# A prologue reordered: the context made during the softmax, the sums of B by TensorE, spare products in TensorE's first pauses, and all loads behind the first x1 on one queue

## The chip, the cores and the metric

The kernel runs on one core of a Trainium2 chip. All arithmetic is float32. The metric is the device time of one execution, in microseconds (us), as the median of several runs. Beside that, one execution was recorded by the profiler; every duration below comes from that record, with times counted from the start of its span.

## The reference, cut to what matters

The input is x with 128 batch rows, 64 channels and 1024 positions, and a conditioning vector of 128 numbers for each batch row. Two layers follow each other, each added to x.

```python
# layer 0
h   = gelu(gelu(cond @ W0 + b0) @ W1 + b1)
att = softmax(h @ W2 + b2)                        # 128 batch rows x 8
agg_w, agg_b = att . weight, att @ bias_k         # a 64x64 matrix and 64 biases for each batch row
z   = agg_w @ x + agg_b                           # for each batch row
x   = x + z @ (A @ B.T).T + ffn_bias              # rank 128
# layer 1
y   = grouped_conv(x, 9 taps, 4 groups) + cond @ c_weight.T + fside      # the middle term is the "context"
x   = x + y @ W_up + the low-rank part of the expert that a gate picks (4 experts, rank 8)
```

The product with B comes first in the kernel: x B is 128 columns wide, the 64x64 matrices act on that, and A widens it again. A bias agg_b that is constant along the positions becomes, after B, agg_b times the column sums of B. That is what the "sums of B" are for.

## The kernel before

Two batch rows make a pair (128 partitions: 64 channels twice), and there are 64 pairs. For each pair, `layer0_in` multiplies the transposed x by B (eight 128x128 products into `pxb`), `layer0_mix` multiplies by a block matrix with the two 64x64 matrices (`pz`), and `layer0_out` multiplies by A (two 128x512 products into `pd`), adds x on VectorE, writes the result to a scratch in DRAM (`x1d`, two transfers) and reads it back shifted into a tile `X` (two transfers), on which the convolution works. `conv_in` makes the convolution for one batch row of a pair (`pc`), and `conv_out` adds the context and writes `yt`. Two pairs make one step d of the last layer: `ffn_a`, `ffn_sums` and `ffn` multiply `yt` by W_up in seven products of sub-blocks (`w11`, `w12`, `w21`, `w22` and the sums T1 to T4 of them that `w_sum` makes).

The engines' instruction orders are written by hand: each engine runs its instructions in the order of the program text, and waits in place for what it needs. Every engine that issues DMAs (SP, ScalarE as ACT, and GpSimd as POOL) issues them in that order too. SP and ACT each have one queue, and POOL has one.

The prologue is the part before the loop over d. It reads the packed parameters (`pk`), B, the x of pair 0, A and others; makes `att` in `condition`; and carries the first four pairs (FIRST = 4) through layer 0 with block matrices that VectorE builds itself from `att` and the weights (`own_att`: a product `pattx` that turns `att` for the pair; `own_bd`: eight steps on VectorE; `own_bias`: the biases, with `attT` from `turn_att`). For all later pairs, `agg_all` makes the 64x64 matrices of all batch rows with eight products, and `agg_out` writes them to DRAM, from where `load_cond` reads them group by group (a group is two pairs). `load_cond` also broadcasts agg_b and the context of the group to all partitions; before, both lie in one scratch, `smalld`, in a tile `bc`, and `condition_rest` makes them. `b_sums` makes the column sums of B with two products from `bred`, a reduction of B over its eight chunks on VectorE (line 598).

Lines that matter later: 197 and 205 (the first products of `condition`), 228 and 232 (`b_sums`), 241 (`pattx`), 220 (`attT`), 258 (steps of the block matrix), 307, 317, 340 (`pxb`, `pz`, `pd`), 341 (x added), 342 (x1d written), 345 and 346 (X read), 187 (`bc` read), 406 (convolution of pairs 0 and 1), 442 (products with W_up), 369 and 370 (differences for the later pairs' convolution, on POOL), 556 (the bias added to x). The main text of the prologue before reads, around pair 0:

```python
    layer0_mix(0, sums_of_b)
    own_att(1)
    own_bd(1)
    small = condition_rest()
    own_bias(1)
    load_x(2, nc.scalar)
    nc.sync.dma_start(smalld, small)
    layer0_out(0)
    load_cond(0)
    load_cond(1)
```

Of the kernel before, what the change touches and what calls it, by code (L numbers as in the profile page):

```python
# [44 lines left out]
GP = 2  # L45
# [23 lines left out]
def block(ctx: ExitStack, tc: tile.TileContext, a: dict, out: bass.AP):  # L69
# [21 lines left out]
    def bank(name):  # L91
        return ps.tile([P, 512], F32, tag="bank", name=name)
# [7 lines left out]
    ident = const.tile([P, P], F32, name="ident")  # L100
    make_identity(nc, ident)

    xs, xts, bds, bcs = {}, {}, {}, {}

    def load_x(pr, eng=nc.gpsimd):
        xts[pr] = xtp.tile([P, NC, P], F32, tag="xt", name=f"xt{pr}")
# [65 lines left out]
    fold = const.tile([P, GL], F32, name="fold")  # L172
    nc.vector.tensor_tensor(fold, ident[:, :GL], ident[:, GT : GT + GL], ALU.add)
    aggd = dram.tile([NB, CH, CH], F32, name="aggd")
    smalld = dram.tile([NB, 2, CH], F32, name="smalld")

    def load_cond(g):

        if g * GP >= FIRST:
            bds[g] = BD[g % NBD]  # L180
            for b in range(2):
                nc.sync.dma_start(
                    bds[g].rearrange("(r two) t b o -> two r t b o", two=2)[b, :, :, b, :],
                    aggd.rearrange("(t two) r o -> two r t o", two=2)[b, :, g * GP : (g + 1) * GP],
                )
        bcs[g] = bcp.tile([P, GP, 2, 2, CH], F32, tag="bc", name=f"bc{g}")
        nc.sync.dma_start(
            bcs[g].rearrange("p t b k o -> p (t b k o)"),
            smalld[2 * g * GP : 2 * (g + 1) * GP]
            .rearrange("b k o -> (b k o)")  # L190
            .unsqueeze(0)
            .partition_broadcast(P),
        )

    def mlp(w, h, b, name):
        p = bank(f"p{name}")
        nc.tensor.matmul(p[:, :NB], w, h, start=True, stop=True)
        o = const.tile([P, NB], F32, tag=name, name=name)
        nc.scalar.activation(o, p[:, :NB], AF.Gelu, bias=b)
        return o  # L200

    def condition():
        h = mlp(w1, mlp(w0, condT, b0, "h0"), b1, "h1")
        p = bank("plogit")
        nc.tensor.matmul(p[:, :8], h, w2, start=True, stop=True)
        lg = const.tile([P, 8], F32, name="lg0")
        nc.vector.tensor_tensor(lg, p[:, :8], b2, ALU.add)
        nmx = const.tile([P, 1], F32, name="nmx")
        nc.vector.tensor_reduce(nmx, lg, AX.X, ALU.max, negate=True)
        ex = const.tile([P, 8], F32, name="ex")  # L210
        nc.scalar.activation(ex, lg, AF.Exp, bias=nmx)
        sm = const.tile([P, 1], F32, name="sm")
        nc.vector.tensor_reduce(sm, ex, AX.X, ALU.add)
        rs = const.tile([P, 1], F32, name="rs")
        nc.vector.reciprocal(rs, sm)
        nc.vector.tensor_scalar(att[:, :, :8], ex.unsqueeze(1).to_broadcast([P, 4, 8]), rs, None, ALU.mult)

    def turn_att():
        p = bank("pattT")
        nc.tensor.transpose(p[:, :P], att.rearrange("p j k -> p (j k)"), ident)  # L220
        nc.scalar.copy(attT, p[:, :P])

    bred = const.tile([P, P], F32, name="bred")

    def b_sums():

        p = bank("pbs8")
        nc.tensor.matmul(p[:8, :P], ones[:, :8], bred, start=True, stop=True)
        nc.scalar.copy(bs8, p[:8, :P])
        yield  # L230
        p = bank("pbsum")
        nc.tensor.matmul(p[:, :1], bred, ones[:, :1], start=True, stop=True)
        nc.scalar.copy(bsum, p[:, :1])
        yield
# [26 lines left out]
    attT = const.tile([P, NB], F32, name="attT")  # L261
    bsum = const.tile([P, 1], F32, name="bsum")

    def condition_rest():

        p = bank("psmall")
        nc.tensor.matmul(p[:, :CH], attT[:8, :], bk, start=True, stop=True)
        nc.tensor.matmul(p[:, CH : 2 * CH], condT, cwT, start=True, stop=True)
        small = const.tile([NB, 2, CH], F32, name="small")
        nc.scalar.copy(small[:, 0], p[:, :CH])  # L270
        nc.vector.tensor_tensor(small[:, 1], p[:, CH : 2 * CH], fs, ALU.add)
        return small

    aggs = []

    def agg_all():

        first = ytp.tile([NB, 4, 512], F32, tag="yt", name="agg0")
        second = [xpool.tile([NB, 2, 512], F32, tag="x", name=f"agg1{j}") for j in range(2)]
        to = aggd.rearrange("b i o -> b (i o)").rearrange("b (j h n) -> h b j n", j=4, h=2)  # L280
        aggs.extend([(to[0], first), (to[1][:, :2], second[0]), (to[1][:, 2:], second[1])])
        for h in range(2):
            ps4 = [psb.tile([P, N], F32, tag=f"pb{j}", name=f"pagg{h}_{j}") for j in range(4)]
# [13 lines left out]
            nc.sync.dma_start(to, agg)  # L297


    xbs, z0s, yts, opened = {}, {}, {}, {}  # L300
    diffs, pms, m2s, pcs = {}, {}, {}, {}

    def layer0_in(pr):
# [5 lines left out]
        nc.scalar.copy(xb, pxb[:, :P])  # L309
        xbs[pr] = xb  # L310

    def layer0_mix(pr, between=None):
# [5 lines left out]
        if between:  # L318
            next(between)
        z0 = z0p.tile([P, P], F32, tag="z0", name=f"z0_{pr}")  # L320
        to = z0.rearrange("k (o b) -> k b o", b=2)
        pzv = pz[:, :P].rearrange("k (b o) -> k b o", b=2)
        if own:
            nc.tensor.matmul(pz[:, :P], bs8, mv[pr].rearrange("k b o -> k (b o)"), start=False, stop=True)
            nc.scalar.copy(to, pzv)  # L325
        else:
            nc.vector.scalar_tensor_tensor(to, bcs[g][:, t, :, 0, :], bsum, pzv, ALU.mult, ALU.add)
        z0s[pr] = z0

    def layer0_out(pr):  # L330
        x, z0 = xs[pr], z0s.pop(pr)
        xt = X[pr % NX]
        d = x1d.tile([Q, P, P], F32, tag="x1d", name=f"x1d{pr}")
        dv = d.rearrange("q (c g) m -> (q c) g m", g=BG)
        h = P // 2
        for hf in range(2):
            cols = slice(hf * 512, (hf + 1) * 512)
            qs = slice(hf * Q // 2, (hf + 1) * Q // 2)
            pd = bank(f"pd{pr}_{hf}")
            nc.tensor.matmul(pd, z0, at[:, cols], start=True, stop=True)  # L340
            nc.vector.tensor_tensor(x[:, cols], pd, x[:, cols], ALU.add)  # L341
# [13 lines left out]
        return v.rearrange("m (g q o) -> m g q o", g=NGC, q=Q)  # L355

    def context(pr, b, rows=slice(0, P)):
        v = bcs[pr // GP][rows, pr % GP, b, 1, :].rearrange("m (g o) -> m g o", g=NGC)
        return v.unsqueeze(2).to_broadcast([v.shape[0], NGC, Q, GC])

    def differences(pr):
# [269 lines left out]
    lb = loaded("lb", [P, N])  # L631
    next(agg)
    own_att(2)
    own_bd(2)
    own_bias(2)
    conv(0)
# [140 lines left out]
```

## Time and profile before

| | |
|---|---|
| median of 3 runs | 1360.44 us (1358.38 to 1361.58) |
| the profiled execution | 1360.38 us, span 1358.6 us |
| TensorE (PE) busy | 1336.9 us, 98% of the span |
| VectorE (DVE), POOL busy | 586.8 us, 622.1 us |
| granted TensorE clock, mean | 0.997 |
| DMA | 189.64 MB, mean 140 GB/s |
| PE busy in 0 to 10, 10 to 20, 20 to 30, 30 to 40 us | 4.28, 10.00, 7.78, 5.58 us |
| PE busy from 200 to 1300 us | 1100.00 us |

PE is TensorE's multiplying, PEld its loading of weights, which runs beside it. A row of the timeline gives the start, the length of a run of like instructions, the engine, the line, the tiles, the shape, and in brackets how long the engine was idle before and what released it. A product in float32 is recorded as two matmuls. A DMA row gives the time from issue to landing at its end. The difference of 1.8 us between the profiled execution's own time and its span lies around the span.

### The profile page before, as it was taken

The page shows a single profiled execution, that of the slowest core. Times are in us where ns is not written, and L with a number is a line of the kernel's source. Part 1 is how long each engine was busy: PE and PEld are TensorE (multiplying, and loading weights), DVE is VectorE, ACT ScalarE, POOL GpSimd, SP SyncE. Part 2 cuts the span into 40 slices and gives each one's busy share as a digit, 9 for nine tenths or more (in the row PEclk, how much of TensorE's full clock was granted, in tenths as well). Part 3 has the DMA queues.
Part 4 walks back from the last instruction along what each step waited for, and adds up shares of the span by engine and source line. Part 5 has one row for each costly group of instructions (what it writes and reads, how often), then busy time and mean ns, then how long its engine had stood idle before and what let it go on. Part 6 is the DMA issues. An engine that isn't in the chain of part 4 may idle for free.

```text
span 1358.6 us, 18209 instructions
## 1 busy us (share of the span) xinstructions
PE 1336.9 (98%) x7279; PEld 757.6 (56%) x7279; DVE 586.8 (43%) x980; ACT 142.4 (10%) x310; POOL 622.1 (46%) x553
## 2 busy tenths in 40 slices
PE   6999999999999999999999999999999999999997
PEld 4655555555455555555555555555555554555553
DVE  6554344344344444343443343443443443444442
ACT  2011011011011011011010111010110110110100
POOL 2454555344554344554345554445553445543322
PEclk9999999999999999999999999999999999999999
DMA  8854454534445444445434545343544344454220
GB/s 297 268 198 134 108 160 134 155 124 125 121 146 154 141 133 118 134 134 165 139 119 128 139 135 164 125 133 107 160 136 152 124 127 123 142 157 142 70 79 31
DMA packets 179541, 189.64 MB, mean 140 GB/s; under 512 B 16640, under 2 KB 148096, under 8 KB 179072
## 3 DMA queue, kind: packets, MB, share of 16 engines
q1 hardware_dynamic: 160592, 119.25, 31.2%
q0 software_dynamic: 17712, 65.02, 13.9%
q10 hardware_dynamic: 1152, 4.19, 0.9%
q8 instruction: 58, 0.95, 0.3%
q14 instruction: 27, 0.22, 0.1%
HBM read 119.16 MB, written 69.27 MB: 139 GB/s over the span
## 4 chain that ended last, share of the span: by engine, by line
PE 96%; DMA 1%; POOL 1%; DVE 1%; issue 0%; ACT 0%; DVEq 0%; SPq 0%; ACTq 0%; POOLq 0%
PE pb L442 56%; PE pxb L307 9%; PE pc L415 9%; PE pd L340 8%; PE pg L473 4%; PE pm L377 4%; PE pb L548 2%; PE pz L317 1%; PE pgt L488 1%; DMA bc<-smalld 1%; PE pc L406 1%; DVE bdx L258 0%; PE pzt L513 0%; POOL df L370 0%; POOL df L369 0%
## 5 line engine op out<-in xcount | busy, mean ns | idle before, releaser
L442 PE MATMUL pb<-wT,s 128*128 128x512 f32 x768 | 346.0, 600 | 0.0
L442 PE MATMUL pb<-w,yt 128*128 128x512 f32 x512 | 230.6, 593 | 0.7 <-ACT v L456 0.7
L442 PEld LDWEIGHTS pb<-wT,s 128*128 128x128 f32 x768 | 140.8, 190 | 158.7 <-issue 158.7
L108 POOL DMA_DIRECT2D xt<-in_xt x60 | 33.1, 552 | 381.5 <-PE pxb L307 365.6
L556 POOL TENSOR_TENSOR x<-x,ffn_bias 128x1024 f32<-128x1024 f32 x63 | 149.2, 2388 | 40.3 <-DMA x<-in_x 40.3
L550 DVE TENSOR_TENSOR x<-pb,x 128x512 f32<-128x512 f32 x96 | 60.3, 684 | 230.2 <-PE pl L548 230.2
L392 DVE TENSOR_TENSOR m<-pm,bc 64x512 f32<-64x512 f32 x124 | 85.0, 685 | 167.0 <-PE pm L377 165.1
L442 PEld LDWEIGHTS pb<-w,yt 128*128 128x128 f32 x512 | 94.8, 190 | 108.5 <-issue 106.8
L341 DVE TENSOR_TENSOR x<-pd,x 128x512 f32<-128x512 f32 x128 | 88.1, 689 | 126.9 <-PE pd L340 126.6
L427 DVE TENSOR_TENSOR yt<-pc,m 128x512 f32<-128x512 f32 x124 | 124.7, 1083 | 22.6 <-PE pc L415 22.6
L340 PE MATMUL pd<-AT,z 128*128 128x512 f32 x256 | 125.6, 613 | 1.4 <-ACT z L325 1.4
L307 PE MATMUL pxb<-B,xt 128*128 128x128 f32 x1024 | 125.7, 282 | 0.0
L307 PEld LDWEIGHTS pxb<-B,xt 128*128 128x128 f32 x1024 | 119.7, 195 | 6.8 <-DVE x L550 5.1
L415 PEld LDWEIGHTS pc<-ws,df 128*64 128x64 f32 x1984 | 107.0, 137 | 27.3 <-issue 23.5
L415 PE MATMUL pc<-ws,df 128*64 128x128 f32 x1984 | 122.0, 276 | 0.0
L442 PE MATMUL pb<-w,s 128*128 128x512 f32 x256 | 115.2, 593 | 0.7 <-DVE x L541 0.7
L442 PE MATMUL pb<-w-T,yt 128*128 128x512 f32 x256 | 115.2, 593 | 0.0
L369 POOL TENSOR_TENSOR df<-X 128x512 f32<-128x512 f32 x62 | 65.4, 1055 | 96.7 <-DMA X<-x1d 94.4
L462 POOL TENSOR_TENSOR s<-yt 128x512 f32<-128x512 f32 x32 | 40.5, 1264 | 147.0 <-DVE yt L427 147.0
L442 PEld LDWEIGHTS pb<-w,s 128*128 128x128 f32 x256 | 48.6, 190 | 62.2 <-issue 60.7
L395 ACT COPY m<-m 64x512 f32<-64x512 f32 x124 | 76.5, 617 | 58.5 <-DVE m L392 55.3
L442 PEld LDWEIGHTS pb<-w-T,yt 128*128 128x128 f32 x256 | 46.1, 190 | 55.2 <-issue 54.9
(111 smaller groups left out, 1154.6 us busy)
## 6 DMA issues: line engine op xcount, KB each, us to landing
x1d<-x SPq DMA_DIRECT2D x128, 256.0 KB, 2.3
X<-x1d SPq DMA_DIRECT2D x128, 256.0 KB, 4.1
out<-x SPq DMA_DIRECT2D x64, 512.0 KB, 2.7
xt<-in_xt POOLq DMA_DIRECT2D x60, 512.0 KB, 3.9
x<-in_x POOLq DMA_DIRECT2D x60, 512.0 KB, 4.6
bc<-smalld SPq DMA_DIRECT2D x32, 256.0 KB, 3.9
w<-in_w SPq DMA_DIRECT2D x2, 1024.0 KB, 8.7
bd<-aggd SPq DMA_DIRECT2D x60, 32.0 KB, 4.0
```

The source lines that it names most:

```text
L307: nc.tensor.matmul(pxb[:, :P], xt[:, c, :], bt[:, c, :], start=(c == 0), stop=(c == NC - 1))
L340: nc.tensor.matmul(pd, z0, at[:, cols], start=True, stop=True)
L341: nc.vector.tensor_tensor(x[:, cols], pd, x[:, cols], ALU.add)
L369: nc.gpsimd.tensor_tensor(diffs[pr][:, :, 0], at_even, at_odd, ALU.subtract)
L377: nc.tensor.matmul(pm[b * H : (b + 1) * H, g * P : (g + 1) * P], blocks(pr, b, g, 1), wsum[:, g], start=True, stop=True,)
L392: nc.vector.tensor_tensor(by_group(m2[half, b]), by_group(pm[half]), context(pr, b, half), ALU.add)
L395: nc.scalar.copy(m2[other, b], m2[half, b])
L415: nc.tensor.matmul(pc[o * H : (o + 1) * H, cols], diffs[pr][:, 2 * g + b, o], ws[:, g, o], start=True, stop=True,)
L427: nc.vector.tensor_tensor(yt.rearrange("m q (o g two) -> m two g q o", two=2, g=NGC)[:, b], by_group(pcs.pop((pr, b))), context(pr, b) if ...
L442: nc.tensor.matmul(to, yt[:, c], w[:, c], start=first and c == 0, stop=c == HC - 1, skip_group_check=not first)
L550: nc.vector.tensor_tensor(x[:, cols], part, x[:, cols], ALU.add)
L556: eng.tensor_tensor(xs[pr], xs[pr], fbias, ALU.add)
```

## The change

The diff, cut to what does work (renamings follow from it):

```diff
-    smalld = dram.tile([NB, 2, CH], F32, name="smalld")
+    ctxd = dram.tile([NB, CH], F32, name="ctxd")
+    aggbd = dram.tile([NB, CH], F32, name="aggbd")
...
-        bcs[g] = bcp.tile([P, GP, 2, 2, CH], F32, tag="bc", name=f"bc{g}")
+            load_rows(g, aggbs, aggbd, "ab")
+        load_rows(g, ctxs, ctxd, "cx")
+
+    def load_rows(g, tiles, src, tag):
+
+        tiles[g] = bcp.tile([P, GP, 2, CH], F32, tag=tag, name=f"{tag}{g}")
         nc.sync.dma_start(
...
+    def spare(j, name):
+
+        return psb.tile([P, N], F32, tag=f"pb{j}", name=name)
+
+    def busy(p, n):
+
+        for _ in range(n):
+            nc.tensor.matmul(p[:, :P], ident, ident, start=True, stop=True)
+
     def condition():
-        h = mlp(w1, mlp(w0, condT, b0, "h0"), b1, "h1")
+        idle = spare(0, "idle")
+        busy(idle, 3)
+        h = mlp(w0, condT, b0, "h0")
+        busy(idle, 1)
+        h = mlp(w1, h, b1, "h1")
+        busy(idle, 1)
...
         nc.scalar.activation(ex, lg, AF.Exp, bias=nmx)
+        context_all()
+        b_row(range(3))
         sm = const.tile([P, 1], F32, name="sm")
...
-    bred = const.tile([P, P], F32, name="bred")
-
-    def b_sums():
-
-        p = bank("pbs8")
-        nc.tensor.matmul(p[:8, :P], ones[:, :8], bred, start=True, stop=True)
-        nc.scalar.copy(bs8, p[:8, :P])
-        yield
-        p = bank("pbsum")
-        nc.tensor.matmul(p[:, :1], bred, ones[:, :1], start=True, stop=True)
+    def b_row(chunks):
+
+        if 0 in chunks:
+            sums_of_b.append(spare(2, "pbs8"))
+        for c in chunks:
+            nc.tensor.matmul(sums_of_b[0][:8, :P], ones[:, :8], bt[:, c], start=c == 0, stop=c == NC - 1)
+        if NC - 1 in chunks:
+            nc.scalar.copy(bs8, sums_of_b[0][:8, :P])
+
+    def b_column():
+
+        p = spare(3, "pbsum")
+        nc.tensor.matmul(p[:, :1], bs8[:1, :], ones[:1, :1], start=True, stop=True)
         nc.scalar.copy(bsum, p[:, :1])
...
-    def condition_rest():
-
-        p = bank("psmall")
+    def context_all():
+
+        p = spare(1, "pctx")
+        nc.tensor.matmul(p[:, :CH], condT, cwT, start=True, stop=True)
+        o = const.tile([NB, CH], F32, name="ctx")
+        nc.vector.tensor_tensor(o, p[:, :CH], fs, ALU.add)
+        nc.sync.dma_start(ctxd, o)
+
+    def agg_b_all():
+        p = bank("paggb")
         nc.tensor.matmul(p[:, :CH], attT[:8, :], bk, start=True, stop=True)
...
+        o = const.tile([NB, CH], F32, name="aggb")
+        nc.scalar.copy(o, p[:, :CH])
+        aggs.append((aggbd, o))
...
-    def layer0_out(pr):
+    def layer0_out(pr, then=None):
...
+        if then:
+            then()
         nc.sync.dma_start(xt[h:, :, :P], dv[:h])
         nc.sync.dma_start(xt[:h, :, 1 : P + 1], dv[h:])
...
-    nc.vector.tensor_reduce(bred, bt.rearrange("p c k -> p k c"), AX.X, ALU.add)
     own_att(0)
+    own_att(1)
     turn_att()
+    b_row(range(3, NC))
     own_bias(0)
     layer0_in(0)
-    sums_of_b = b_sums()
-    next(sums_of_b)
     own_bd(0)
     add_fbias(0, nc.vector)
-    layer0_mix(0, sums_of_b)
-    own_att(1)
+    layer0_mix(0)
+    b_column()
+    agg_b_all()
+    layer0_out(0, lambda: load_x(2, nc.sync))
     own_bd(1)
-    small = condition_rest()
+    add_fbias(1, nc.vector)
     own_bias(1)
-    load_x(2, nc.scalar)
-    nc.sync.dma_start(smalld, small)
-    layer0_out(0)
     load_cond(0)
-    load_cond(1)
-
-    add_fbias(1, nc.gpsimd)
+    load_w("11", nc.sync)
+
     add_fbias(2, nc.gpsimd)
-    load_w("11", nc.gpsimd)
-    load_w12(nc.gpsimd)
     layer0_in(1)
     agg = agg_all()
     next(agg)
     layer0_mix(1)
-    layer0_out(1)
+    own_att(2)
+
+    def rest():
+        load_w("21", nc.sync)
+        load_cond(1)
+
+    layer0_out(1, rest)
+    load_w12(nc.sync)
     load_w("22", nc.sync)
-    load_w("21", nc.sync)
     load_x(3, nc.sync)
     gl = loaded("gl", [P, NC, GT])
     lb = loaded("lb", [P, N])
+    add_fbias(3, nc.gpsimd)
     next(agg)
-    own_att(2)
     own_bd(2)
     own_bias(2)
     conv(0)
...
     layer0(2)
-    add_fbias(3, nc.gpsimd)
+    v = ffn_a(0)
     w_sum("T1", "12", "11")
+    conv(1)
     w_sum("T2", "22", "T1")
-    v = ffn_a(0)
-    conv(1)
     load_x(4)
```

In words: `load_cond` reads agg_b and the context from two scratches, agg_b only for groups that need it. The context is made and written while the softmax still runs. The sums of B are eight products that accumulate over B's chunks, three of them before `att` is turned and five after, and the column form of the sums comes from the row form. Five products of the identity with itself, whose result nobody reads, stand before and between the products of the conditioning network. The loads of x for pair 2 and of w11 and w12 move to SP's queue, each at a stated place between the transfers of x1d and X. Pair 0's x is added ahead of the building of pair 1's block matrix, and pair 1's bias is added by VectorE.

More of the change, by code (lines that the diff above doesn't have):

```diff
@@ L101, in block @@
     make_identity(nc, ident)
-    xs, xts, bds, bcs = {}, {}, {}, {}
+    xs, xts, bds, aggbs, ctxs = {}, {}, {}, {}, {}
     def load_x(pr, eng=nc.gpsimd):
@@ L185, in load_cond @@
                 )
-        bcs[g] = bcp.tile([P, GP, 2, 2, CH], F32, tag="bc", name=f"bc{g}")
+            load_rows(g, aggbs, aggbd, "ab")
+        load_rows(g, ctxs, ctxd, "cx")
+    def load_rows(g, tiles, src, tag):
+        tiles[g] = bcp.tile([P, GP, 2, CH], F32, tag=tag, name=f"{tag}{g}")
         nc.sync.dma_start(
[L188 to L192, printed above, removed]
+            tiles[g].rearrange("p t b o -> p (t b o)"),
+            src[2 * g * GP : 2 * (g + 1) * GP].rearrange("b o -> (b o)").unsqueeze(0).partition_broadcast(P),
         )
@@ L221, in turn_att @@
         nc.scalar.copy(attT, p[:, :P])
-    bred = const.tile([P, P], F32, name="bred")
-    def b_sums():
-        p = bank("pbs8")
-        nc.tensor.matmul(p[:8, :P], ones[:, :8], bred, start=True, stop=True)
-        nc.scalar.copy(bs8, p[:8, :P])
-        yield
-        p = bank("pbsum")
-        nc.tensor.matmul(p[:, :1], bred, ones[:, :1], start=True, stop=True)
+    def b_row(chunks):
[8 more added lines that the diff above has]
+        nc.tensor.matmul(p[:, :1], bs8[:1, :], ones[:1, :1], start=True, stop=True)
         nc.scalar.copy(bsum, p[:, :1])
-        yield
     attx, bdx, mv = {}, {}, {}
@@ L262, in block @@
     bsum = const.tile([P, 1], F32, name="bsum")
-    def condition_rest():
-        p = bank("psmall")
-        nc.tensor.matmul(p[:, :CH], attT[:8, :], bk, start=True, stop=True)
[L268 to L272, printed above, removed]
+    def context_all():
[6 more added lines that the diff above has]
+        p = bank("paggb")
+        nc.tensor.matmul(p[:, :CH], attT[:8, :], bk, start=True, stop=True)
+        o = const.tile([NB, CH], F32, name="aggb")
+        nc.scalar.copy(o, p[:, :CH])
+        aggs.append((aggbd, o))
     aggs = []
@@ L282, in agg_all @@
         for h in range(2):
-            ps4 = [psb.tile([P, N], F32, tag=f"pb{j}", name=f"pagg{h}_{j}") for j in range(4)]
+            ps4 = [spare(j, f"pagg{h}_{j}") for j in range(4)]
             for j in range(4):
@@ L297, in agg_out @@
             nc.sync.dma_start(to, agg)
-    xbs, z0s, yts, opened = {}, {}, {}, {}
+    xbs, z0s, yts, opened, sums_of_b = {}, {}, {}, {}, []
     diffs, pms, m2s, pcs = {}, {}, {}, {}
@@ L310, in layer0_in, with layer0_mix @@
         xbs[pr] = xb
-    def layer0_mix(pr, between=None):
+    def layer0_mix(pr):
         g, t = pr // GP, pr % GP
@@ L317, in layer0_mix @@
         nc.tensor.matmul(pz[:, :P], xbs.pop(pr), bd.rearrange("p b o -> p (b o)"), start=True, stop=not own)
-        if between:
-            next(between)
         z0 = z0p.tile([P, P], F32, tag="z0", name=f"z0_{pr}")
@@ L326, in layer0_mix @@
         else:
-            nc.vector.scalar_tensor_tensor(to, bcs[g][:, t, :, 0, :], bsum, pzv, ALU.mult, ALU.add)
+            nc.vector.scalar_tensor_tensor(to, aggbs[g][:, t], bsum, pzv, ALU.mult, ALU.add)
         z0s[pr] = z0
-    def layer0_out(pr):
+    def layer0_out(pr, then=None):
         x, z0 = xs[pr], z0s.pop(pr)
@@ L357, in context @@
     def context(pr, b, rows=slice(0, P)):
-        v = bcs[pr // GP][rows, pr % GP, b, 1, :].rearrange("m (g o) -> m g o", g=NGC)
+        v = ctxs[pr // GP][rows, pr % GP, b].rearrange("m (g o) -> m g o", g=NGC)
         return v.unsqueeze(2).to_broadcast([v.shape[0], NGC, Q, GC])
```

## The prediction

> **What bounds the kernel now.** I read the page's busy rows first, then busy time by stage, then TensorE's (PE's) timeline through the prologue, the chain of waits, and last the DMA issues one by one.
>
> ```profile
> span 1358.6 us, 18209 instructions
> PE 1336.9 (98%) x7279; PEld 757.6 (56%) x7279; DVE 586.8 (43%) x980; ACT 142.4 (10%) x310; POOL 622.1 (46%) x553
> ```
>
> ```profile
> 0.00:10.00 10.00, 4.28 (x15) 3.43 (x16) 4.27 (x14) 4.66 (x9) 2.06 (x18) 1.00 0.82 290
> ...
> 20.00:30.00 10.00, 7.78 (x42) 4.51 (x41) 6.26 (x13) 3.46 (x10) 4.03 (x4) 1.00 0.78 258
> 30.00:40.00 10.00, 5.58 (x64) 5.49 (x64) 3.30 (x8) 0.07 (x1) 0.00 (x0) 0.66 0.84 244
> 40.00:50.00 10.00, 9.17 (x48) 5.48 (x46) 8.43 (x15) 1.03 (x3) 0.34 (x1) 1.00 1.01 380
> ...
> 200.00:1300.00 1100.00, 1100.00 (x6049) 622.85 (x6048) 464.91 (x772) 112.73 (x241) 512.34 (x447) 1.00 0.46 135
> ```
>
> Columns: stretch, length, busy PE, PEld, DVE, ACT, POOL, granted clock, DMA share, GB/s. From 200 to 1300 us PE has no idle time, so nothing to win there; the change doesn't alter its work. What can be won lies in the first 60 us, and the stretch 30 to 40 stands out: PE half idle, at a granted clock of 0.66.
>
> ```profile
> 8.71 3.75 PE L307 MATMUL pxb<-B,xt 128*128 128x128 f32 x16
> ...
> 16.20 3.73 PE L340 MATMUL pd<-AT,z 128*128 128x512 f32 x4
> 19.72 2.79 PE L307 MATMUL pxb<-B,xt 128*128 128x128 f32 x16
> ...
> 24.94 1.98 PE L340 MATMUL pd<-AT,z 128*128 128x512 f32 x4 [0.53 <-ACT z L325]
> ...
> 34.42 5.70 PE L406 MATMUL pc<-ws,X 128*64 128x128 f32 x64 [6.10 <-DMA bc<-smalld]
> ...
> 49.40 3.72 PE L406 MATMUL pc<-ws,X 128*64 128x128 f32 x64
> ```
>
> Two losses show. PE waits 6.10 us before pair 0's convolution, which then runs in 5.70 where pair 1's takes 3.72: cold clock, 1.98 more. And everything up to about 21.5 us is cold too (pd 3.73 against 1.98 later), although the clock column says 1.00 there; durations decide.
>
> ```profile
> 16.90 2.33 DVE bdx L258
> ...
> 20.51 1.21 DVE x L341 x2
> 21.71 0.02 issue
> 21.73 2.33 DMA x1d<-x
> ...
> 24.70 9.72 DMA bc<-smalld
> 34.43 5.69 PE pc L406 x64
> ```
>
> This is the chain into the wait. Pair 0's x (L341) is added only after pair 1's block matrix (L258), one step of which took 2.33 instead of 0.36 beside POOL's addition (POOL at L556, 16.61 to 19.07). Then come x1d, X and bc. The chain names bc, but PE waits on X as well: its second half was issued at 24.08 and took
>
> ```profile
> X<-x1d SPq DMA_DIRECT2D x1, 256.0 KB, 10.1
> ```
>
> so it landed at 34.2; pair 3's, with less beside it, took 4.1. What lay beside the first were the 2 MB of w11 and w12, issued by POOL from 23.84.
>
> **The change, part by part, on this execution's clock.**
>
> Spare products: five 128x128 products. A cold one costs 0.456 (3.65 us of the chain for eight pxb). Three stand ahead of pk's landing (3.04), from about 1.3: 1.4 us, covered. One stands in each gelu gap (0.46 each): covered to within 0.1. Without cover, 5 x 0.456 = 2.3 us.
>
> Context early: product and add (0.69 PE, 0.22 DVE) go into DVE's 0.60 us wait for the exponential: nothing; uncovered, 0.9.
>
> Sums of B: DVE's reduction (L598, 1.89) and one product (0.53) go; eight products come. B lands at 2.09 + 5.2 = 7.29. Three products run to 8.66, though att is ready for pattx at 7.91: +0.75 (bounds: 0.1 warm, 1.1 if B lands 0.35 later). Then pattx twice and pattT to 9.9, five products to 12.2. pxb(0) starts at 12.2, not 8.71: 3.5 us later. DVE, free of the reduction, has bdx(0) at 12.95 (before 12.74) and x0's bias at 14.15.
>
> The clock. [...] The row: PE is busy from 7.91 without a pause, yet pd at 16.2 is still cold. [...] Then pxb(0) ends at 15.3, and 1.71 later (as from 42.34 to 44.05) pd(0) starts, at 17.0 instead of 16.2, but runs 1.98, not 3.73. pbsum and agg_b's product sit in the gap for z0's copy (0.4).
>
> DVE order: x0's adds now precede bdx(1), at 18.1 and 19.05 to 19.75 instead of 20.51 to 21.71: 2.0 us earlier. bdx(1) then runs 19.75 to 22.7 (2.96, no POOL beside it), x1's bias on DVE (1.22) to 23.95. PE: pxb(1) to 20.9, pagg to 22.0, waits 0.75 for bdx(1), pd(1) 24.05 to 26.05 (pattx(2), moved ahead of it, lies in the gap for z1's copy), pagg to 27.15.
>
> X of pair 0: x1d issued at 18.85 and 19.8, landed (2.2, 2.3) 21.05 and 22.1. xt2 and x2 now stand on SP between them and X: two issues (0.9 us, done before 21.05) and 1 MB, 2.5 us at the 400 GB/s of bulk loads, data 21.8 to 24.4. X's 0.5 MB at the 250 GB/s of pair 3's stage ends 26.4, landed 26.9. So the convolution starts at 27.15 with PE hardly idle, not 34.43: 7.3 us, and runs warm: 1.98. Sum 9.2.
>
> All of this rests on X staying ahead of w11. Row: x1d of pair 2, issued at 46.0 behind 3.5 MB on the same queue, landed after 5.6, behind lb (40.6 + 10.3). One queue keeps its order; two queues cost X 6 us. [...] Then X would still take 10.1, landing at 32.3; PE idle 5.1, cold again, and only 2.1 of the 9.2 are left. I follow the row.
>
> Loads behind. From 26.4 on one queue at 410 GB/s: cx0 0.4, w11 2.5 (29.3; wanted 36.8), x1d1 1.3, w21 2.5, cx1 0.4, X1 2.0 (36; wanted 40), w12 2.5 (38.5; w_sum's halves are wanted at 38 and 39), w22 2.5 (41; 45), xt3 and x3 2.5: x3 lands at 43.4 (before 49.6, so 6.2 earlier where PE is 9.2 earlier). Issue time: xt2 and x2 leave ACT (0.8 us), w11 and w12 leave POOL (1.75), none of it on the path; SP has 3 us without work before x1d1 for w11, and w21 and cx1 are out before X1's wait for x1d1 ends. SP's waits for an older transfer meet landed ones. If the rate is 10% lower, each is 1.5 to 2 late, w12 first; it holds up DVE, and pair 1's convolution outputs now stand ahead of T2.
> gl and lb, then x1d2 landed at 46.1, X2 issued 46.1; wanted by pm at 54.75. Alone 4 to 5.5 us; POOL's four loads (2 MB, from 47.3) repeat X0's collision: up to 10.1, 56.8. Cost 0 to 2; I take 0 (most of X2 goes ahead).
>
> POOL: x3's bias 43.4 to 47.3 (3.94 as before), then loads, wsum and sums as before, 8.43, to 55.8. The differences of pair 2 want to start at 64.12 - 9.2 = 54.9 (wT releases the buffer). 0.9 late, less 0.1 slack: PE's 0.68 wait at 80.24 grows by 0.8.
>
> Later: each group's load is two DMAs instead of one, 31 issues of 0.5 us on SP, hidden since PE is saturated and they stand behind X; aggb's write is one more issue before aggd. Uncovered at most 15 us, but there is no PE wait for it to lengthen. Order elsewhere is unchanged.
>
> Sum: 7.3 + 1.9 - 0.8 = 8.4. The profiled execution took 1360.38 (span 1358.6 and 1.8 around it); the median of runs is 1360.44, the same. 1360.4 - 8.4 = 1352.0.
>
> **The rivals.**
> (1) Warm by 11.2: pxb(0) ends at 13.6, all 1.7 earlier: 1350.3. [...]
> (2) [...]warm near 21: pd(0) 17.65 to 21.25, convolution at 29.4: 5.0 + 2.0, POOL less late, -0.5: 6.5, 1353.9. [...]
> (3) X interleaves with loads wherever they are issued: 2.1 left, 1358.3.
> (4) Slower: one queue too slow, pair 2's X late. 7.6 MB stand between X0 and x1d2's landing. To be slower than before, X2 must land after 63.95, so x1d2 after some 59.5: 33 us, under 230 GB/s. For: 30 to 40 us moved 244. Against: 40 to 50, mostly one queue, 380. At 200 GB/s: 64.4 + 4.1 = 68.5, 4.5 late: 1365.
>
> **How the numbers follow.** Main case 0.50; (1) 0.13; (2) 0.24; (3) 0.08; (4) 0.05. 0.2%, about what a measurement of this kernel can tell from no change, is 2.7 us: (3) is split between same and faster. Faster 0.91, same 0.04, slower 0.05. The range takes in the main case, (1), (2) and the bounds (sums 0.35, X2 2.0, rate 2[...]): 1348.5 to 1357.
>
> **What would show it.** pd(0) near 2 us long rather than 3.7, at about 17; the convolution of pair 0 starting before 29 and taking 3.7; X of pair 0 landing within 5 us; no stretch with clock 0.5 around 32; pg (62.17 before) near 53; PE's wait at 80.24 reappearing near 71 with 1 to 1.5 us. Wrong if x1d or X of pair 0 take over 8 us with nothing of POOL's beside them, if DVE reaches x0's adds after 21, or if PE waits for w12's sum or X2 by over 3 us.

## The result, and the profile after

| | before | after |
|---|---|---|
| median of 10 runs each, on one chip | 1360.28 us (1358.38 to 1363.67) | 1357.33 us (1356.24 to 1358.97) |
| ratio after to before, 95% interval | | 0.9976 [0.9966, 0.9986] |
| the profiled execution | 1360.38 us, span 1358.6 | 1357.43 us, span 1355.7 |

The kernel became faster, by 2.9 us instead of the 8.4 forecast; 1357.33 lies just above the top of the range. The first view is the page's busy rows, the second busy time by stage of the kernel after (columns as before: stretch, length, busy PE, PEld, DVE, ACT, POOL, granted clock, DMA share, GB/s).

```profile
span 1355.7 us, 18254 instructions
PE 1337.9 (99%) x7303; PEld 756.3 (56%) x7303; DVE 585.8 (43%) x980; ACT 142.5 (11%) x310; POOL 619.7 (46%) x549
```

```profile
20.00:30.00 10.00, 7.47 (x33) 2.90 (x34) 7.42 (x16) 3.37 (x10) 2.35 (x1) 0.83 1.04 299
30.00:40.00 10.00, 9.17 (x92) 7.14 (x89) 8.31 (x20) 0.80 (x4) 0.00 (x0) 1.00 1.07 300
...
50.00:60.00 10.00, 8.58 (x60) 5.55 (x59) 5.06 (x5) 0.91 (x3) 9.90 (x9) 1.00 0.87 261
60.00:70.00 10.00, 9.95 (x27) 4.33 (x25) 9.76 (x10) 1.24 (x2) 10.00 (x6) 1.00 0.78 225
70.00:80.00 10.00, 6.62 (x15) 2.82 (x16) 2.64 (x5) 0.27 (x1) 7.68 (x8) 1.00 0.56 193
200.00:1300.00 1100.00, 1100.00 (x6049) 622.69 (x6048) 464.56 (x772) 113.83 (x242) 514.08 (x448) 1.00 0.46 135
```

The last ten of these first 80 us in the kernel before:

```profile
70.00:80.00 10.00, 9.57 (x23) 3.86 (x21) 6.11 (x11) 0.52 (x2) 10.00 (x9) 1.00 0.48 178
```

The hole that was at 30 to 40 us is closed: PE is busy 9.17 us there instead of 5.58. A new one has opened at 70 to 80 us, where PE has 6.62 us (before: 9.57), and in the two stretches ahead of it POOL is busy nearly all the time. From 200 us on nothing has changed. PE's timeline through the prologue of the kernel after shows both:

```profile
12.30 2.52 PE L333 MATMUL pxb<-B,xt 128*128 128x128 f32 x16
...
16.43 1.98 PE L364 MATMUL pd<-AT,z 128*128 128x512 f32 x4
...
22.20 0.46 PE L343 MATMUL pz<-bdx,xb 128*128 128x128 f32 x2 [0.92 <-DVE bdx L279]
...
23.43 3.68 PE L364 MATMUL pd<-AT,z 128*128 128x512 f32 x4
...
29.74 3.72 PE L432 MATMUL pc<-ws,X 128*64 128x128 f32 x64 [1.56 <-DMA X<-x1d]
...
55.52 1.95 PE L499 MATMUL pg<-yt,gl 128*64 128x256 f32 x16
...
58.93 3.70 PE L468 MATMUL pb<-wT,s 128*128 128x512 f32 x8 [0.59 <-POOL s L489]
...
71.44 0.33 PE L539 MATMUL pzt<-ident,zm 128*128 128x128 f32 x1 [1.49 <-DVE zm L529]
72.04 3.70 PE L468 MATMUL pb<-w-T,yt 128*128 128x512 f32 x8 [0.27 <-DVE u L561]
77.41 3.70 PE L468 MATMUL pb<-w,s 128*128 128x512 f32 x8 [1.68 <-DVE x L567]
```

The same two points of the kernel before, from its PE timeline:

```profile
62.17 1.95 PE L473 MATMUL pg<-yt,gl 128*64 128x256 f32 x16
...
80.24 3.70 PE L442 MATMUL pb<-w,s 128*128 128x512 f32 x8 [0.68 <-DVE x L541]
```

At `pg` the kernel after is 6.65 us ahead (62.17 to 55.52). At the product with `w` and `s` (called P3 below) it is 2.83 ahead (80.24 to 77.41), which is what the spans differ by (2.9). So the front did win most of what was expected, and 3.8 us were lost again between `pg` and P3: waits of 0.59, 1.49, 0.27 and 1.68 us where before had only 0.68.

P3 waits for x of the first step. VectorE's part of that (line 567) waits in turn for the last of POOL's additions to x (line 564; 538 before):

```profile
76.67 0.69 DVE L567 TENSOR_TENSOR x<-pb,x 128x512 f32<-128x512 f32 x1 [4.68 <-POOL x L564]
```

POOL's timeline of the kernel after:

```profile
47.87 4.05 POOL L582 TENSOR_TENSOR x<-x,ffn_bias 128x1024 f32<-128x1024 f32 x1 [20.16 <-DMA x<-in_x]
51.87 0.70 POOL L108 DMA_DIRECT2D xt<-in_xt  x1
...
56.74 2.14 POOL L489 TENSOR_TENSOR s<-s,yt 128x512 f32<-128x512 f32 x1
58.84 2.26 POOL L490 TENSOR_TENSOR s<-yt 128x512 f32<-128x512 f32 x1
61.05 3.32 POOL L491 TENSOR_TENSOR s<-yt,s 128x512 f32<-128x512 f32 x1
64.33 1.03 POOL L395 TENSOR_TENSOR df<-X 128x512 f32<-128x512 f32 x1
...
75.38 1.26 POOL L564 TENSOR_TENSOR x<-x,u 128x512 f32<-128x512 f32 x1
```

And of the kernel before:

```profile
49.66 3.94 POOL L556 TENSOR_TENSOR x<-x,ffn_bias 128x1024 f32<-128x1024 f32 x1 [24.07 <-DMA x<-in_x]
...
60.70 1.27 POOL L465 TENSOR_TENSOR s<-yt,s 128x512 f32<-128x512 f32 x1
64.19 1.95 POOL L369 TENSOR_TENSOR df<-X 128x512 f32<-128x512 f32 x1 [2.22 <-DVE wT L150]
```

This is the reading that matters. POOL begins with x3's bias when x3 has landed, and then has a row of work without a pause: that bias, four loads, `wsum`, four sums, and the differences `df` of the next pair. Before, POOL was done with the sums at 61.97 and idled for 2.22 us until VectorE released the buffer for `df`; that release follows `pg`, by 2.0 us. POOL was early, PE's place set the time. After, the release would come near 57.5 (55.52 + 2.0), but POOL is free only at 64.33, no bracket, no idle time: POOL is late, and its `df` starts no earlier than before (64.19). x3 landed only 1.8 us earlier than before, and three of the sums, now beside VectorE's T3 and its negative, took 2.14, 2.26 and 3.32 us instead of 1.26 each. Before, those same two operations of VectorE met `df`, which took 1.95 and 3.08 us instead of 1.03. From x3's bias to its last addition POOL thus works for 27.6 us before and 28.8 after, so once its idle time is used up, the landing of x3 sets P3.

### The profile page after: what moved, and what is told of

Its sections match the earlier page's. It is cut to its first block, busy times and chain, and to the rows that moved or that the text cites. A ratio compares the mean times of both kernels' runs of the same rounds, so it can differ in the third digit from the quotient of the medians.

```text
span 1355.7 us, 18254 instructions
## 1 busy us (share of the span) xinstructions
PE 1337.9 (99%) x7303; PEld 756.3 (56%) x7303; DVE 585.8 (43%) x980; ACT 142.5 (11%) x310; POOL 619.7 (46%) x549
## 3 DMA queue, kind: packets, MB, share of 16 engines
q1 hardware_dynamic: 165776, 122.14, 32.1%
q10 hardware_dynamic: 864, 3.15, 0.6%
## 4 chain that ended last, share of the span: by engine, by line
PE 95%; issue 2%; POOL 2%; DMA 1%; DVE 0%; SPq 0%; DVEq 0%; ACT 0%; POOLq 0%; ACTq 0%
PE pb L468 56%; PE pc L441 9%; PE pxb L333 9%; PE pd L364 8%; PE pg L499 4%; PE pm L403 4%; PE pb L574 2%; PE pz L343 1%; PE pgt L514 1%; POOL x L582 1%; DMA B<-in_B 0%; DMA x<-in_x 0%; PE pbs L247 0%; PE pzt L539 0%; POOL s L491 0%
## 5 line engine op out<-in xcount | busy, mean ns | idle before, releaser
L418 DVE TENSOR_TENSOR m<-pm,cx 64x512 f32<-64x512 f32 x124 | 85.0, 685 | 167.0 <-PE pm L403 165.1
L441 PEld LDWEIGHTS pc<-ws,df 128*64 128x64 f32 x1984 | 107.0, 137 | 27.3 <-issue 23.5
L488 POOL TENSOR_TENSOR s<-yt 128x512 f32<-128x512 f32 x32 | 40.6, 1268 | 149.3 <-DVE yt L453 149.3
L468 PEld LDWEIGHTS pb<-w-T,yt 128*128 128x128 f32 x256 | 46.1, 190 | 55.3 <-issue 54.9
```

Source lines behind the costliest of these rows:

```text
L418: nc.vector.tensor_tensor(by_group(m2[half, b]), by_group(pm[half]), context(pr, b, half), ALU.add)
L441: nc.tensor.matmul(pc[o * H : (o + 1) * H, cols], diffs[pr][:, 2 * g + b, o], ws[:, g, o], start=True, stop=True,)
L468: nc.tensor.matmul(to, yt[:, c], w[:, c], start=first and c == 0, stop=c == HC - 1, skip_group_check=not first)
```

## The experiments

Eleven kernels, each an edit of the kernel after and timed beside the kernel before (1360.29 to 1360.63 us there). Three theories are weighed. P: POOL's in-order wait for x3 holds up the sums behind it, so it is enough to take that wait out of POOL. D: POOL and VectorE stretch each other when they work side by side, whatever the transfers do. V: the prologue's transfers, one behind another, decide when x3 and X are there, and all else follows.

One table first, of the profiled executions. "`df` wanted" is the start of `pg` + 2.0; "last addition" is the end of line 564 on POOL; P3 is the product above, with its own length beyond 3.7 us in brackets where it ran longer. Such products are called cold below, and the others warm, by their length: in before the granted clock was 0.50 from 32 to 38 us, where pair 0's convolution took 5.70 us instead of 3.72, and in after 0.50 from 24 to 26.5 us, where pair 1's `pd` took 3.68 instead of 1.98. For the cold products of the other kernels no granted clock is shown. In a2 and e3 `df` waited for pair 2's X; in a1 the bias is VectorE's.

| kernel | x3's bias starts | `df` wanted | `df` starts | last addition | P3 starts | span |
|---|---|---|---|---|---|---|
| before | 49.66 | 64.2 | 64.19 | 79.46 | 80.24 | 1358.6 |
| after | 47.87 | 57.5 | 64.33 | 76.64 | 77.41 | 1355.7 |
| a1, x3's bias on VectorE | | 58.7 | 58.92 | 77.49 | 78.27 (+2.9) | 1359.4 |
| a2, x3 ahead of w12 | 42.91 | 58.4 | 61.39 | 74.13 | 76.79 | 1354.9 |
| a3, no spare products | 48.33 | 57.9 | 64.69 | 76.99 | 77.77 | 1356.0 |
| a4, x2 behind X | 50.94 | 57.6 | 65.69 | 77.99 | 78.78 (+1.7) | 1358.7 |
| c1, 2 MB less | 42.93 | 57.9 | 57.97 | 73.21 | 73.99 | 1352.4 |
| c2, x4 and x5 on SP | 48.46 | 58.1 | 59.66 | 75.02 | 75.80 | 1354.3 |
| c3, w11 and w12 on POOL | 50.97 | 59.6 | 66.28 | 78.59 | 79.36 | 1357.8 |
| d1, a2 and c2 | 42.38 | 58.1 | 58.17 | 73.80 | 74.58 | 1353.1 |
| e1, a4 and d1 | 40.45 | 54.9 | 56.02 | 72.30 | 73.08 (+1.7) | 1353.3 |
| e2, e1 and spare products | 44.86 | 59.4 | 60.45 | 77.39 | 78.17 | 1356.7 |
| e3, sums of B on VectorE | 44.92 | 56.1 | 59.75 | 72.39 | 76.85 | 1355.0 |

P3 starts 0.77 to 0.79 us behind POOL's last addition in every row but a2's and e3's, where PE itself arrives later. And the start of P3, with the excess in its length, gives the span: d1 is 5.66 ahead of before at P3 and 5.5 in the span, e1 7.16 less 1.7 and 5.3. Nothing behind 85 us changes these differences by more than 0.3 us.

**The front: spare products and sums of B.** Kernel a3 leaves the five spare products out:

```diff
-        busy(idle, 3)
         h = mlp(w0, condT, b0, "h0")
-        busy(idle, 1)
         h = mlp(w1, h, b1, "h1")
-        busy(idle, 1)
```

> The changed kernel without its five spare products. If the spare products bring the early clock: [...]pd of pair 0 starts 1 to 3 us later, X0 lands later by as much, the time is up by 0.5 to 2 us. [...]

Measured: 1357.90 us, ratio 0.9981 [0.9974, 0.9988], against 0.9976 of the kernel after. Pair 0's `pd` took 1.98 us at 16.81, as warm as with the spare products. Beside the sums of B they change nothing that can be measured.

Kernel e3 gives the sums of B back to VectorE's reduction and one product (the column form still comes from the row form), with all else of the change kept:

```diff
-        b_row(range(3))
...
+    nc.vector.tensor_reduce(bred, bt.rearrange("p c k -> p k c"), AX.X, ALU.add)
...
-    b_row(range(3, NC))
     own_bias(0)
     layer0_in(0)
+    b_row(range(NC))
```

> The changed kernel with the sums of B made as before: VectorE's reduction over the chunks and one product, behind pxb of pair 0. If the eight products pay for themselves by the early clock: pxb(0) starts 3 us earlier but cold, [...]pd(0) ends within 0.7 us of where it did, time unchanged within 0.7 us. If the clock comes early anyhow: pd(0) 2 to 3 us earlier, X0 earlier by as much, time 0 to 1.5 us less. If the reduction delays VectorE's block matrix: 0.5 to 1 us more.

Measured: 1356.60 us (1354.19 to 1361.41), 0.9973 [0.9966, 0.9980]. `pxb` of pair 0 started at 8.89 instead of 12.30, its `pd` at 14.31 instead of 16.43 and warm (1.98 us), `pg` at 54.13 instead of 55.52. So the eight products cost some 2 us at the front, and with the spare products in place `pd` took 1.98 us without them as well; the change without either was not tried. But of the 2 us only 1.4 were left at `pg`, because pair 0's convolution, after a wait of 2.32 us for X, ran cold (5.39 us), and 0.6 at P3, no more than the intervals can tell from nothing. In between stands

```profile
54.13 1.95 PE L497 MATMUL pg<-yt,gl 128*64 128x256 f32 x16
59.73 1.10 PE L401 MATMUL pm<-wsum,X 128*64 128x128 f32 x16 [3.65 <-DMA X<-x1d]
60.76 5.40 PE L466 MATMUL pb<-wT,s 128*128 128x512 f32 x8
```

In this PE timeline of e3 the bracket is pair 2's X: PE was early, the transfer was not (issued at 47.61 and 48.29, beside POOL's 2 MB of x4 and x5 from 47.22; PE went on 11.4 us after the second issue, where in the kernel after the second half landed 4.5 us after its own), and after 3.65 us of waiting the next product with W_up ran in 5.40 instead of 3.70.

**POOL's wait for x3 (theory P).** Kernel a1 gives x3's bias to VectorE behind T2, and puts POOL's loads of x4 and x5 behind its sums:

```diff
-    add_fbias(3, nc.gpsimd)
...
     w_sum("T2", "22", "T1")
-    load_x(4)
-    load_x(5)
+    add_fbias(3, nc.vector)
...
         s = ffn_sums(d)
+        if d == 0:
+            load_x(4)
+            load_x(5)
```

> The changed kernel, with pair 3's bias added by VectorE after T2 instead of by POOL, and POOL's loads of x4 and x5 behind its four sums, so that POOL no longer stands waiting for x3. Theory P (POOL's serial chain, which begins when x3 lands at 47.8 us, sets when PE may go on at 77.4): POOL's sums begin when yt is there, near 47.5, and end near 52.5; PE's waits between 58 and 77 (4.0 us in all) nearly vanish; 3 to 4 us less than the changed kernel, about 1353.5 us. Theory D (PE's waits come from VectorE, whose steps are stretched beside POOL whatever POOL waits for; more work for VectorE can't help): within 1 us of the changed kernel, 1356.5 to 1358.

Measured: 1360.19 us, 0.9998 [0.9989, 1.0007]: the whole gain was gone. POOL's timeline and PE's P3 in a1:

```profile
56.64 0.70 POOL L108 DMA_DIRECT2D xt<-in_xt  x1
...
67.87 2.35 POOL L582 TENSOR_TENSOR x<-x,ffn_bias 128x1024 f32<-128x1024 f32 x1 [1.69 <-DMA x<-in_x]
71.79 1.04 POOL L395 TENSOR_TENSOR df<-X 128x512 f32<-128x512 f32 x1 [1.57 <-DMA X<-x1d]
```

```profile
78.27 6.60 PE L468 MATMUL pb<-w,s 128*128 128x512 f32 x8 [4.23 <-DVE x L567]
```

The sums were indeed done at 56.64 and not at 64.33, so POOL's wait was real. But the loads of x4 and x5 were now issued 5 us later, at 56.64 to 58.4 where the kernel after has 51.87 to 53.6. x5's bias waited for its landing, pair 3's `df` for X, POOL's last addition ended at 77.49, later than in the kernel after, and P3 ran cold. Neither forecast held. P in its simple form falls; the edit moved two things at once, and what it shows is that the next transfer takes the place of the wait removed. Of its lateness 1.2 us lie ahead of all this: in this execution X of pair 0 landed later, and `pg` with it (56.73).

**x3 earlier.** Kernel a2 issues the load of x3 ahead of w12 and w22 (the transposed xt3 stays behind them):

```diff
+    xs[3] = xpool.tile([P, L], F32, tag="x", name="x3")
+    nc.sync.dma_start(xs[3], a["x"][3])
     load_w12(nc.sync)
     load_w("22", nc.sync)
-    load_x(3, nc.sync)
+    xts[3] = xtp.tile([P, NC, P], F32, tag="xt", name="xt3")
+    nc.sync.dma_start(xts[3], a["xt"][3])
```

> The changed kernel, with the load of x3 (not of its transposed copy xt3) moved ahead of w12 and w22 on SP's queue; nothing else. Theory P: x3 lands near 42 instead of 47.8, POOL's chain starts that much earlier, the four sums begin when yt is there (47.5); 2.5 to 4 us less than the changed kernel, about 1354. T1 and T2 wait about 1.3 us longer for w12 and w22, which VectorE's slack hides. Theory D: no change within 1 us. Against both: POOL's loads of x4 and x5 now start near 44.5 and may hold up X of pair 2 beyond 57; then PE waits at pm.

Measured: 1356.80 us, 0.9968 [0.9957, 0.9979], better than after by 0.5 us (medians) to 1.1 us (ratios); the two intervals overlap, so this gain is not shown. x3's bias ran at 42.91, in 2.36 us (4.05 in after, beside VectorE). P3's wait was gone. In its place PE waited 2.99 us for pair 2's X at 61.37: POOL, early now, issued its 2 MB from 45.21, ahead of X (56.17).

**x2 behind the read of X.** Kernel a4 moves the load of x2 from between x1d and X to behind X and the context:

```diff
-    layer0_out(0, lambda: load_x(2, nc.sync))
+    layer0_out(0)
...
     load_cond(0)
+    load_x(2, nc.sync)
     load_w("11", nc.sync)
```

> The changed kernel, with the load of xt2 and x2 moved behind the read of X0 and the context on SP's queue. X0 should land near 26 instead of 29.5, and the convolution of pair 0 start when PE is ready, near 28.3 instead of 29.74. Theory P: the time hardly moves (within 0.7 us), because x3 lands when it did and POOL's chain hangs on it. Rival (the convolution's start carries through to the end): 1.4 us less.

Measured: 1360.04 us, 0.9992 [0.9984, 1.0000]. The local aim was met: the second half of X of pair 0 took 4.6 us instead of 7.8, and PE did not wait for it. Yet the result is 2.7 us worse than after, which neither forecast had: x3's bias starts at 50.94, 3 us later (1 us of it because this execution's front was late, `pd` of pair 0 at 17.48 instead of 16.43), and the table's row follows from there. An earlier convolution is worth nothing when POOL's row of work behind x3 sets P3.

**Less to transfer (theory V against D).** Kernel c1 takes 2 MB off the queue: w12 becomes a copy on ScalarE from w11, W22 is W21 (so the products with these two use other weights):

```diff
-            eng.dma_start(W12[h], a["w12"][:, h * HC // 2 : (h + 1) * HC // 2])
+            nc.scalar.copy(W12[h], W["11"][:, h * HC // 2 : (h + 1) * HC // 2])
...
-    load_w("22", nc.sync)
+    W["22"] = W["21"]
```

> The changed kernel with 2 MB less to load: w12 is replaced by a copy of w11 that ScalarE makes in its idle time, w22 by w21, so that the output lacks the true w12 and w22; every instruction on the four computing engines is otherwise as before. Theory V (the transfers of the prologue, one behind the other, set when x3, X of pair 2 and x5 are there, and POOL's chain follows): x3 lands near 43 instead of 47.8, X of pair 2 near 49, PE's waits between 58 and 77 vanish, 3 to 4 us less than the changed kernel, about 1353.7. Theory D (the additions on POOL and the sums on VectorE stretch each other, whatever lands when): within 1 us of the changed kernel.

Measured: 1354.63 us (1353.93 to 1354.78), 0.9955 [0.9943, 0.9967]. PE's timeline of c1, at the same two points as above:

```profile
55.91 1.95 PE L499 MATMUL pg<-yt,gl 128*64 128x256 f32 x16
...
73.99 3.70 PE L468 MATMUL pb<-w,s 128*128 128x512 f32 x8 [0.68 <-DVE x L567]
```

`pg` is no earlier than in the kernel after, so the front won no more: 6.26 us. But now P3 is 6.25 us ahead of before and its wait is back at before's 0.68. All that `pg` gained goes through to the end. VectorE and POOL do the same additions as in after, in the same order, and still meet: one of POOL's sums took 3.21 us. But the sums were done at 55.77, 2.2 us before `df` was wanted. So D does not explain the loss without x3's late landing: here the same stretching falls where POOL has time to spare.

**x4 and x5 on SP's queue.** Kernel c2 has SP issue the loads of x4 and x5 behind pair 2's X, so POOL issues none of them:

```diff
     layer0(2)
+    load_x(4, nc.sync)
+    load_x(5, nc.sync)
...
-    load_x(4)
-    load_x(5)
```

> The changed kernel, with the loads of x4, xt4, x5 and xt5 issued by SP behind the read of pair 2's X instead of by POOL behind pair 3's bias. POOL loses 2.3 us of issuing in its chain and the loads start some 1 us earlier, behind X and not beside it. Theory V with POOL's chain as the last link: 1.5 to 2.5 us less than the changed kernel, about 1355.3. If x5 or X of pair 3 lands last instead: no more than 0.7 us less.

Measured: 1355.92 us (1355.10 to 1356.06), 0.9965 [0.9952, 0.9977]. POOL saves 2.3 us of issuing, its sums end before VectorE's T3 meets most of them (only the fourth took 2.25 us), and `df` starts at 59.66 instead of 64.33.

**w11 and w12 back on POOL's queue.** Kernel c3 asks what the one queue is worth:

```diff
-    load_w("11", nc.sync)
     add_fbias(2, nc.gpsimd)
+    load_w("11", nc.gpsimd)
+    load_w12(nc.gpsimd)
...
-    load_w12(nc.sync)
```

> The changed kernel, with w11 and w12 issued by POOL again, behind pair 2's bias as before the change; all else stays. If one queue keeps X0 ahead of the weights and two queues mix: POOL issues them only after x2 has landed (25.4 + 2.4), so X0 is nearly through and lands as it did, near 29.5; X1, read near 33, is the one that now mixes with 2 MB and lands near 42 to 43 instead of 40.6. The time: within 1.5 us of the changed kernel. If the queue is indifferent: no change at all in X1's landing.

Measured: 1359.53 us, 0.9994 [0.9985, 1.0003], so some 2 us of after's 2.9 hang on where these two are issued, more than the 1.5 expected. The DMA issues of c3: X of pair 1, first half, issued at 31.60 beside POOL's 2 MB from 29.58,

```profile
X<-x1d SPq DMA_DIRECT2D x1, 256.0 KB, 11.6
```

and of the kernel after, X of pair 1, second half, issued at 33.56 with everything on SP's queue:

```profile
X<-x1d SPq DMA_DIRECT2D x1, 256.0 KB, 7.0
```

The half shown landed at 43.2 in c3 and at 40.6 in the kernel after (the views give no time for the other half); in c3 the convolution of pair 1 waited 1.08 us, and x3's bias came at 50.97. Whether such a load passes X c3 can't show by itself, since w12 is issued there ahead of X (30.28) and in the kernel after behind it (34.13). The kernel before can, as X and these loads lay on two queues: w12's first half, issued by POOL at 24.54, landed at 31.7, ahead of X's second half, issued by SP at 24.08 and landed at 34.2. On the one queue of the kernel after w11, issued 1.2 us behind X, landed 2.6 us behind it (29.5 and 32.1). So on two queues a load issued 0.5 us behind X landed 2.5 us ahead of it, and on one queue the load stayed behind.

**Both at once.** Kernel d1 is a2 and c2 together: x3 ahead of w12, and x4, x5 behind pair 2's X on SP.

> Both: x3's load ahead of w12 and w22, and x4 and x5 loaded by SP behind pair 2's X. By theory V no transfer that POOL's chain or PE needs is late: POOL adds pair 3's bias near 43 to 45.5, makes its sums as soon as yt is there (48.5), X of pair 2 lands near 54, before pm at 57; the waits of PE between 58 and 77 vanish: 4 us less than the changed kernel, about 1353.4, better than either. By theory D: 1356.5 or more.

Measured: 1354.20 us (1353.94 to 1354.84), 0.9953 [0.9941, 0.9966]. This is the version to keep: 6.4 us ahead of before beside it, and some 3 ahead of after. Its POOL timeline shows the row of work in order again:

```profile
42.38 2.37 POOL L582 TENSOR_TENSOR x<-x,ffn_bias 128x1024 f32<-128x1024 f32 x1 [13.57 <-DMA w<-in_w]
...
58.17 1.96 POOL L395 TENSOR_TENSOR df<-X 128x512 f32<-128x512 f32 x1 [1.16 <-DVE wT L150]
```

As before the change, POOL waits for VectorE's release (1.16 us), and that follows PE. The same bytes in another order recover what c1 recovered with 2 MB less. It takes both moves: x3 alone (a2) made X of pair 2 late, and x4 and x5 alone (c2) left x3 late. So it is the order of the transfers, not the volume as such.

**More at the front.** Kernel e1 is d1 with a4's edit on top; e2 adds four spare products ahead of pair 1's `pz`, against the cold `pd` of pair 1 (in the kernel after the granted clock fell to 0.50 for some 3.4 us behind PE's pause of 0.92 us, and `pd` took 3.68 us instead of 1.98):

```diff
     next(agg)
+    busy(bank("idle1"), 4)
     layer0_mix(1)
```

> The version with x3 early and x4, x5 on SP, and besides xt2 and x2 loaded behind X0 and the context. With x3 no longer the last link, the convolution's start should carry through: X0 near 26, the convolution of pair 0 when PE is ready (28.3), 1.2 to 1.6 us less than the version without it: about 1352.9. If x2 and x3, then 2.5 us later each, become the last link again (x3 45 instead of 42.4): the same as without it within 0.6, about 1354.2.

> The same, with four spare products in PE's pause of 0.9 us before pz of pair 1[...]. If the fall is due to that pause and PE's readiness sets the convolution's start: [...]the convolution up to 1.7 us earlier, a gain of 0.5 to 1.5 us. If X0 sets it, or the fall has another cause: no change within 0.5.

Measured: e1 1357.49 us (1354.04 to 1359.90), 0.9980 [0.9972, 0.9989]; e2 1360.57 us, 1.0001 [0.9991, 1.0010]. Both missed. In e1's profiled execution (1355.03) the convolution was at 26.76 without a wait and `pg` at 52.94, 3.2 us ahead of d1's, but P3 only 1.5 ahead, behind a wait of 2.20 us, and cold:

```profile
73.08 5.40 PE L468 MATMUL pb<-w,s 128*128 128x512 f32 x8 [2.20 <-DVE x L567]
```

Here x3 was not the limit: POOL's sums waited 3.09 us for `yt`, began at 48.11, and two of them took 3.15 and 2.25 us beside VectorE, so that `df` came 1.1 us after it was wanted; later POOL waited 0.89 us for VectorE's `zm`. With x3 out of the way, the meeting of the two engines was the next limit in this execution.

In e2's profiled execution (1358.43) pair 1's `pd` did take 1.98 us; but it took 1.98 to 1.99 in a1, c3 and e3 too, with the pause left open, so this does not show what the spare products did. And there PE waited 1.05 and 2.11 us for X of pairs 0 and 1, and x3's bias came at 44.86 instead of 40.45. The medians of e1 and e2 lie 2.5 and 2.1 us above their profiled executions, where d1's executions all lie within 0.9 us. Why, no trace here shows; it stays open.

## Why the prediction was right and wrong

**The front and the clock: right.** `pxb` of pair 0 at 12.30 (12.2 forecast), its `pd` at 16.43 in 1.98 us (17.0, 1.98), x0's adds from 17.60 to 19.14 (18.1 to 19.75), PE's wait for pair 1's block matrix 0.92 (0.75), the convolution of pair 0 in 3.72 instead of 5.70. Rivals (1) and (2), which moved the clock, did not come. The time at which the clock would rise was the author's estimate, and no run shows what sets it: `pxb` of pair 0 took 2.32 to 3.54 us in other kernels with the same front, and pair 0's `pd` took 1.98 to 1.99 in all. Not foreseen: pair 1's `pd` ran cold, 3.68 instead of 1.98. PE's next wait absorbed it, as X was later still.

**"X's 0.5 MB at the 250 GB/s of pair 3's stage ends 26.4, landed 26.9": 2.6 us too early.** The second half was issued at 21.71 and took

```profile
X<-x1d SPq DMA_DIRECT2D x1, 256.0 KB, 7.8
```

so it landed at 29.5. xt2 and x2, put ahead of X, landed at 25.25, near the forecast (data through at 24.4). The mis-sized term is X's own 0.5 MB: from there it took 4.3 us with w11 and the context behind it, where the sum gave 2.5 to the landing. In a4, without x2 ahead, its second half still took 4.6 from issue. This leaves 6.65 of 9.2 at `pg`.

**"From 26.4 on one queue at 410 GB/s ... x3 lands at 43.4": the step that failed.** x3 was issued at 37.09 and took

```profile
x<-in_x SPq DMA_DIRECT2D x1, 512.0 KB, 10.7
```

which is 47.8, 4.4 us late. The bulk rate was right: from the landing of X of pair 1 (33.56 + 7.0 = 40.6) to x3's lie w12, w22, xt3 and x3, 3 MB in 7.2 us (7.5 forecast), and between these two landings the engines moved 402 GB/s. What was too fast is the time up to X of pair 1, which the sum had at 36: 2.6 us of that delay came with X of pair 0, and 2.0 between 34 and 39 us, when X of pair 1 and the context were read. The kernel after, by stage:

```profile
34.00:39.00 5.00, 4.17 (x23) 2.93 (x23) 3.71 (x11) 0.54 (x2) 0.00 (x0) 1.00 1.09 214
49.00:51.00 2.00, 2.00 (x13) 1.45 (x12) 0.71 (x1) 0.00 (x0) 2.00 (x1) 1.00 0.09 27
```

214 GB/s with the DMA engines busy all the time (share 1.09), not 250 and certainly not the 410 that the sum gave to what was mixed in. The second row is a hole of the opposite kind: SP waits for pair 2's x1d, and behind that wait nothing is queued.

**"To 55.8 ... 0.9 late ... PE's 0.68 wait grows by 0.8": the right mechanism, the wrong size.** The row of POOL's work behind x3 was named, with the release that `df` wants at 54.9. `df` came at 64.33, 8.5 later than forecast: 4.5 from x3's landing, and 4.0 from the four sums (9.0 us together), which the forecast took at the durations of before (5.05), when VectorE idled beside them. Against the release, itself 2.6 later than forecast, that is 6.8 late. Of the lateness 3.8 us reached P3, since `df` then took 1.03 instead of 1.95 and 3.08. c1, with x3 at 42.93, had no loss at all after `pg`.

The bill: 2.6 short at X, 3.0 more than the 0.8 lost after `pg`, 5.6 together, against 8.4 - 2.9 = 5.5. The first could not have been recovered by a better X alone, as a4 shows: with POOL late, the end hangs on x3.

**The rivals.** (3), transfers that interleave whoever issues them, gave 1358.3, near the result in number, but not by its mechanism: X took 7.8 and not 10.1, PE waited 1.56 and not 5.1, the convolution was warm. c3 has a piece of what (3) described, with two queues. (4), one queue too slow, named the right resource, but the wrong victim: X of pair 2 was in time in the kernel after (it was late in a2, a4, c3 and e3), and x3 was not.

**Costed at nothing:** the spare products, rightly (a3), and the later pairs' split loads, rightly (PE is busy for all of 200 to 1300 us). The context made during the softmax was not tried by itself. The 3.5 us that the sums of B were to cost at `pxb` were 3.59, of which e3 wins back 2.1 at `pd` and 0.6 at P3.

## What to carry to other kernels

When a stage is moved forward by 9 us, list for every engine that feeds the next stage when its own first input lands, and count that engine's work from there; an engine that idled before (POOL's 2.22 us) had only that much to give. On the one queue here the order of issue was the order of landing (in the kernel after w22 at 45.3, xt3 at 46.6, x3 at 47.8), so put each load by the time at which its consumer's whole row of work must begin: x3 was last of these because its own use is late, but behind its bias stood four loads and five additions, and then `df`. Size a stretch that mixes such loads with reads like X's by a rate measured in such a stretch (214 GB/s here), not by the rate of bulk loads (402), and try the order of transfers before removing work.

## What the runs showed of the hardware that was not expected

- The clock fell behind one short pause. In the kernel after PE idled 0.92 us ahead of pair 1's small products at 22.20, and the next `pd` took 3.68 us instead of 1.98; busy time by stage shows the granted clock:

```profile
19.00:23.00 4.00, 3.08 (x23) 1.91 (x23) 3.75 (x10) 1.34 (x3) 0.00 (x0) 1.00 0.90 266
23.00:27.00 4.00, 3.96 (x7) 1.39 (x6) 2.15 (x5) 0.27 (x1) 1.64 (x1) 0.57 1.13 273
```

  In quarters of a microsecond the clock was 0.50 to 0.59 from 23.5 to 27.0, some 3.4 us in all. With the same pause (0.92 or 0.93 us) the same `pd` took 1.98 to 1.99 in a1, c3 and e3, and 2.70 (a2) to 3.68 (a3) in the others that kept it. What decides between them is not shown.
- Longer waits differ in the same way: after 2.20 us (e1), 2.94 (a4) and 3.65 (e3) the next eight products with W_up took 5.40 instead of 3.70, and after 4.23 (a1) 6.60; after 2.86 (e2) and 2.99 (a2) they took 3.70. Pair 0's convolution was cold after 2.32 us (e3) and warm after 2.65 (c3) and 3.00 (a1).
- Executions whose instructions up to there are the same drift apart at the front: in a1 the first product with B began at 7.89 (7.44 in after), `pxb` of pair 0 took 3.53 us (2.52), and the convolution of pair 0, which waited for X in both, began at 30.95 (29.74).
- Additions of 128x512 on POOL took 1.26 us each in before, with VectorE idle, and up to 3.32 in after beside VectorE's; VectorE's two halves of a sum of W took 2.35 us in before and 3.73 in after.
